# Softmax attention: the value products of two tiles issued as one block in every second step

## The chip, the cores and the metric

The kernel runs on one core of one Trainium2 chip. The metric is the device time of one execution, in microseconds (us). Five engines work side by side, each through its own instructions in the order in which the program issues them: PE (TensorE: matmuls and transposes, results in PSUM), DVE (VectorE), ACT (ScalarE), POOL (GpSimd) and SP (SyncE, which issues the DMAs here). They wait for each other through semaphores.

## The reference, cut to what matters

The whole computation is a chain of six residual blocks on `x` of shape (2, 1024, 128): a mixture of experts, a softmax attention, the same mixture again, a local attention with a feed-forward part, a linear attention, and the local block again. The change touches the softmax attention alone, with 16 heads of 64:

```python
qkv = (x @ qkv_w.T).reshape(Bb, Ss, 3, H, D)
q = _rope(q, c, s)
k = _rope(k, c, s)
scores = jnp.einsum('bhqd,bhkd->bhqk', q, k) * SCALE
dist = jnp.abs(pos[None, :] - pos[:, None])
kb = -p * jnp.log1p(a * dist)
attn = jax.nn.softmax(scores + kb[None], axis=-1)
out = jnp.einsum('bhqk,bhkd->bhqd', attn, v)
return out @ out_w.T
```

## The kernel before, in words

All data are float32. The attention (`attention0`, line 327) walks through 128 steps (line 737): four groups of four heads, two batches, two pairs of heads in a group, and eight tiles of 128 queries. One step is one pair of heads (r = 0 and 1) and one tile of queries against all 1024 keys. The 16 steps of one group and batch are called a block here. The loop (line 752) is a software pipeline written out by hand: nothing reorders it, so each engine gets its instructions in the order of the calls. In step i these calls are made, and each puts work on the engines named:

- `scores_of` (L642, PE): scores of step i. Each head's 1024 scores fill two banks of PSUM (`bank2`), and the two heads take all four banks of pool `psA`, so the scores of step i+1 can start in a bank only after step i's have been read from it.
- `weigh` (L709, PE): products of probabilities and values, for two query tiles at once (256 columns). The keys come in two halves, g = 0 and g = 1, of four key blocks; both halves add up in one bank, "O0". Half g = 0 of a pair of tiles is issued three steps behind the second tile's scores, and half g = 1 four steps behind. So an even step issues a g = 0, and the odd step after it the g = 1 of the same pair.
- `maxima` (L658, DVE): for each head, add the distance bias and take the row maximum, from PSUM into the tile `p`. It ends the use of the score banks.
- `raised` (L671, ACT): the exponential, in place in `p`, with the row sum in `den`.
- `turned` (L692 on PE, then L696 on ACT for head 0 or L698 on DVE for head 1): four 128x128 transposes of step i-2's `p` into one bank (`bankT`), and the copy of the bank into the tile `pt`, which `weigh` reads. A step makes four such calls, (g, r) = (0,0), (0,1), (1,0), (1,1). Pool `psT` has two banks, taken in turn: (1,0) takes the bank of (0,0) after ACT has copied it, and (1,1) takes the bank of (0,1) after DVE has copied it.
- `summed` (L723, ACT): copies the finished products of a pair of tiles from bank O0 into `at`.
- filler between the transposes (0,1) and (1,0): in steps divisible by 4 the output product `project` (L730 on PE, L734 on DVE); in the others one of twelve units for the next block, which are either rotary units (L590 on PE, L601 on DVE, L606 and L607 on POOL, DMAs of L611 on SP) or value projections (L620 on PE, L627 on ACT). In the last block (steps 112 to 127) no next block exists, and pieces of the next mixture of experts (`beside_last`) stand there instead, in some steps only.
- `scale_of` (L676 on DVE, L678 on POOL): divides `p` by its sum.

In 28 of the steps a part of the distance bias is made for a later pair of heads: a logarithm on ACT (L573) and a product on DVE (L574), both issued at the very head of the step. Of these steps 21 are odd (3, 5, 7, 27, 29, 31, 35, 37, 39 and so on) and 7 even.

Of the kernel before, what the change touches and what calls it, by code (L numbers as in the profile page):

```python
# [8 lines left out]
F32 = mybir.dt.float32  # L9
# [5 lines left out]
P = 128  # L15
# [16 lines left out]
def macaron_kernel(ctx: ExitStack, tc: tile.TileContext, a: dict, out: bass.AP):  # L32
    nc = tc.nc

    def pool(name, bufs, stack=ctx, **kw):
        return stack.enter_context(tc.tile_pool(name=name, bufs=bufs, **kw))
# [13 lines left out]
    def bankT(name):  # L50
        return psT.tile([P, 512], F32, tag="T", name=name)
# [3 lines left out]
    def bankO(name, which=None):  # L55
        if which is None:
            turn[0] ^= 1
            which = turn[0]
        return psO.tile([P, 512], F32, tag=f"O{which}", name=name)
# [253 lines left out]
    def beside_last(i):  # L313


        if i is None:
            first_weights()
            return
        for c, s in ((0, 0), (1, 5)):
            if 0 <= i - s < 10:  # L320
                lo, hi = ((0, 1), (1, 3), (3, 4), (4, 5), (5, 7), (7, 9), (9, 10), (10, 11), (11, 12), (12, 13))[i - s]
                for fn, *more in m1[1][3][lo:hi]:
                    fn(c, *more)
        for fn in m1[2][-(-len(m1[2]) * i // 16) : -(-len(m1[2]) * (i + 1) // 16)]:
            fn()

    def attention0():
        with ExitStack() as st:
# [306 lines left out]
            probs, nms, dens, pts, ats, avs = {}, {}, {}, {}, {}, {}  # L635
# [15 lines left out]
            def maxima(i, pss, hp, b, t, bias):  # L651

                o = 896 - t * P
                dens[i] = small.tile([P, 2], F32, tag="den", name=f"den_{hp}_{b}_{t}")
                nms[i] = small.tile([P, 2], F32, tag="nm", name=f"nm_{hp}_{b}_{t}")
                for r in range(2):
                    s = probs[i, r] = sp.tile([P, S], F32, tag="s", name=f"p_{hp}_{b}_{t}_{r}")
                    nc.vector.tensor_tensor_reduce(  # L658
                        out=s,
                        in0=pss[r].rearrange("p a n -> p (a n)"),  # L660
                        in1=bias[r][:, o : o + S],
                        scale=-1.0,
                        scalar=3.0e38,
                        op0=ALU.add,
                        op1=ALU.min,
                        accum_out=nms[i][:, r : r + 1],
                    )

            def raised(i, r):
                s, nm, den = probs[i, r], nms[i], dens[i]  # L670
                nc.scalar.activation(s, s, AF.Exp, bias=nm[:, r : r + 1], scale=-1.0, accum_out=den[:, r : r + 1])  # L671
# [8 lines left out]
            def turned(i, g, r, hp, b, t):  # L680

                q = t % 2
                if q == 0:
                    pts[i // 2, r, g] = work.tile(
                        [P, 4, 2 * P], F32, tag=f"pt{r}{g}", name=f"pt{r}{g}_{hp}_{b}_{t}", bufs=1 + g
                    )
                pt = pts[i // 2, r, g]
                s = probs[i, r]
                tp = bankT(f"tp_{hp}_{b}_{t}_{r}_{g}")
                for k in range(4):  # L690
                    kb = 4 * g + k
                    nc.tensor.transpose(tp[:, k * P : (k + 1) * P], s[:, kb * P : (kb + 1) * P], ident)  # L692
                dst = pt[:, :, q * P : (q + 1) * P]
                src = tp.rearrange("p (k n) -> p k n", n=P)
                if r == 0:
                    nc.scalar.copy(dst, src)  # L696
                else:
                    nc.vector.tensor_copy(dst, src)  # L698
                if g == 1:
                    probs.pop((i, r))  # L700

            def weigh(i, g, hp, b, t, v):

                if g == 0:
                    avs[i // 2] = bankO(f"av_{hp}_{b}_{t}", 0)
                po = avs[i // 2]
                for kb in range(4 * g, 4 * g + 4):
                    for r in range(2):
                        nc.tensor.matmul(  # L709
                            po[r * 64 : r * 64 + 64, 0 : 2 * P],  # L710
                            lhsT=v[:, kb, r * 64 : r * 64 + 64],
                            rhs=pts[i // 2, r, g][:, kb - 4 * g, :],
                            start=(kb == 0),
                            stop=(kb == TB - 1),
                        )
                for r in range(2):
                    pts.pop((i // 2, r, g))

            def summed(i, hp, b, t):
                if t % 4 == 1:  # L720
                    ats[i // 4] = work.tile([P, 4 * P], F32, tag="at", name=f"at_{hp}_{b}_{t}", bufs=1)
                o = 256 * (t % 4 == 3)
                nc.scalar.copy(ats[i // 4][:, o : o + 2 * P], avs.pop(i // 2)[:, 0 : 2 * P])  # L723

# [13 lines left out]
            blocks = {0: block_of(*order[0])}  # L738
            biases, making = {}, {}

            def bias_part(hp, r, *half):
                if hp not in biases:
                    biases[hp], making[hp] = bias_of(hp)
                making[hp](r, *half)
# [3 lines left out]
            work = pool("wk0", 2, st, reuse_waits="tile")  # L748
            sp = pool("sp0", 6, st, reuse_waits="tile")

            with tc.manual_schedule():
                for i in range(len(steps) + 8):
                    def of(d):
                        if 0 <= i - d < len(steps):
                            hg, b, j, t = steps[i - d]
                            return 2 * hg + j, b, t

                    if i == len(steps) - 16:
                        making_stack.close()
                        beside_last(None)  # L760
                    c, e = of(0), of(2)

                    if c:
                        hg, b, j, t = steps[i]
                        for hp, js, places in ((2 * hg + 2, (1, 1), (3, 5, 6, 7)), (2 * hg + 1, (0, 0), (3, 4, 5, 7))):
                            if (b, j) == js and t in places and (hg + 1 < H0 // 4 or not b):
                                k = places.index(t)
                                bias_part(hp, k // 2, slice(k % 2 * WIDE // 2, (k % 2 + 1) * WIDE // 2))
                        pss = scores_of(i, 0, *c, *blocks[i // 16][0][j]) if i else firsts

                    for d, g in ((3, 0), (4, 1)):
                        w = of(d)
                        if w and w[2] % 2 == 1:
                            weigh(i - d, g, *w, blocks[(i - d) // 16][1][w[0] % 2])
                    if c:
                        maxima(i, pss, *c, biases[c[0]])
                        raised(i, 0)
                    if e:
                        turned(i - 2, 0, 0, *e)
                    if c:  # L780
                        raised(i, 1)
                    w = of(4)
                    if w and w[2] % 2 == 1:
                        summed(i - 4, *w)
                    if e:
                        turned(i - 2, 0, 1, *e)

                    if i % 4 == 0 and of(8):
                        project(i - 8, *of(5))
                    elif i == 1:  # L790
                        ap2(0)
                        up2(0)
                        ap2(1)
                    elif 0 < i < len(steps):
                        n = i // 16 + 1
                        if i == 2:
                            up2(1)
                        if n < len(order) and n not in blocks:
                            blocks[n] = block_of(*order[n])
                        if n < len(order) and blocks[n][2]:  # L800
                            blocks[n][2].pop(0)()
                    if len(steps) > i >= len(steps) - 16:
                        beside_last(i - len(steps) + 16)
                    if e:
                        turned(i - 2, 1, 0, *e)
                        turned(i - 2, 1, 1, *e)
                    if c:
                        scale_of(i)
                    if i == 0:
                        rest_of_norm()  # L810
# [133 lines left out]
    work = pool("wk1", 1, reuse_waits="tile")  # L944
# [622 lines left out]
    _, left, finish, front_parts, pair_parts = m1[1]  # L1567
# [115 lines left out]
```

## Time and profile before

| what | value |
|---|---|
| time, median of 3 runs (lowest, highest) | 1916.71 us (1916.43, 1918.86) |
| the profiled execution: its time | 1920.34 us |
| the profiled execution: span from first to last instruction | 1918.6 us |
| mean granted TensorE clock | 0.986 |
| first and last score matmul of the attention (L642) | 135.2 and 990.4 us |
| DVE, ACT, POOL busy, share of the span | 73%, 59%, 59% |

In a timeline each row has the start in us from the span's start, the duration in us, the engine, the line, the operation, the tiles written and read with their shapes, and the number of instructions merged into the row. Brackets hold the idle time of the engine before the row and what ended it. A float32 matmul is issued as two instructions, a transpose as one: a step's four score matmuls are a row of x8, and one half of the value products (eight matmuls) is a row of x16. The ends of PE's rows are modelled and overlap the next start a little, so PE's time is best read from start to start.

### The profile page before, as it was taken

Reading aid. Unit: us, or ns where it says so; the run is one execution under the profiler, and the core shown is the slowest. Engines: PE = TensorE matmul, PEld = TensorE weight load, DVE = VectorE, ACT = ScalarE, POOL = GpSimd, SP = SyncE. Lnnn points to the kernel's source line nnn. Section 1 sums busy time; section 2 is a strip of 40 time slices with the busy share of each in tenths; the row PEclk is TensorE's granted clock in tenths of the full one; section 3 lists DMA queues with packets and bytes.
Section 4 is the critical chain, followed back from the end, with each engine's and each line's share of the span. In section 5 each row is a group of like instructions: output and inputs, shape, how many; then the busy total and the mean of one; then the engine's idle time right before and its main releaser. Section 6 shows DMA issues by size and latency. Waiting matters only on the chain.

```text
span 1918.6 us, 37580 instructions
## 1 busy us (share of the span) xinstructions
PE 1837.8 (96%) x14482; PEld 1190.8 (62%) x14482; DVE 1402.5 (73%) x2450; ACT 1131.1 (59%) x2083; POOL 1135.9 (59%) x1036
## 2 busy tenths in 40 slices
PE   8998999999999999999999888999999899999997
PEld 5554666566665666566566556666756566666665
DVE  5758677776778677776763568888887888888884
ACT  3335555655566555655653356776767467677765
POOL 4544444353434444344444379888887689788883
PEclk8998999999999999999999899999999999999999
DMA  5330101010101101012012111101100000011110
GB/s 132 106 88 23 23 12 34 12 24 11 34 12 23 23 16 30 12 32 62 2 61 98 63 39 29 26 20 29 26 18 15 6 18 18 21 26 24 26 34 26
DMA packets 52413, 64.13 MB, mean 33 GB/s; under 512 B 17890, under 2 KB 26892, under 8 KB 51980
## 3 DMA queue, kind: packets, MB, share of 16 engines
q1 hardware_dynamic: 52236, 61.74, 12.6%
q8 instruction: 115, 1.88, 0.4%
q14 instruction: 62, 0.51, 0.1%
HBM read 27.89 MB, written 1.31 MB: 15 GB/s over the span
## 4 chain that ended last, share of the span: by engine, by line
PE 66%; ACT 12%; DVE 12%; POOL 4%; issue 4%; DMA 0%; SPq 0%; DVEq 0%; POOLq 0%; ACTq 0%
PE s L642 10%; PE tp L692 10%; PE av L709 9%; ACT p L671 4%; PE qk_f L979 3%; PE gu_m L275 3%; PE gu_m L276 2%; PE av_f L1151 2%; PE s_f L1090 2%; PE pq L590 2%; PE tq_f L1046 2%; PE tp_f L1137 2%; PE acc_m L259 2%; PE v_f L1057 2%; PE po_f L1267 2%
## 5 line engine op out<-in xcount | busy, mean ns | idle before, releaser
L678 POOL TENSOR_SCALAR p<-p,den 128x1024 f32<-128x1024 f32 x256 | 293.3, 1160 | 402.8 <-DVE den L676 324.8
L671 ACT ACTIVATE p<-p,nm 128x1024 f32<-128x1024 f32 x256 | 294.7, 1151 | 357.5 <-DVE nm L658 343.9
L658 DVE CUSTOM_DVE_ANT_0 p<-s,bias 128x1024 f32<-128x1024 f32 x256 | 302.8, 1219 | 107.6 <-PE s L642 105.0
L692 PEld LDWEIGHTS tp<-ident,p 128*128 128x128 f32 x2048 | 225.6, 141 | 102.3 <-ACT pt L696 38.7
L692 PE MATMUL tp<-ident,p 128*128 128x128 f32 x2048 | 275.3, 277 | 13.6 <-ACT pt L696 12.8
L642 PE MATMUL s<-qk,qk 64*128 64x512 f32 x1024 | 258.5, 621 | 4.2 <-DVE nm L658 4.2
L709 PE MATMUL av<-pt,v 128*64 128x256 f32 x2048 | 249.0, 385 | 0.0
L698 DVE COPY pt<-tp 128x512 f32<-128x512 f32 x256 | 176.2, 688 | 90.9 <-PE tp L692 90.5
L709 PEld LDWEIGHTS av<-pt,v 128*64 128x64 f32 x2048 | 135.7, 136 | 150.1 <-issue 83.7
L1025 POOL TENSOR_TENSOR t_f<-t_f,t_f 128x1024 f32<-128x1024 f32 x64 | 151.2, 2363 | 15.3 <-DVE t_f L1011 12.5
L299 POOL TENSOR_TENSOR h_m<-h_m,cb_m 128x512 f32<-128x512 f32 x64 | 87.2, 1364 | 120.3 <-DVE h_m L295 90.5
L696 ACT COPY pt<-tp 128x512 f32<-128x512 f32 x256 | 147.7, 577 | 4.9 <-PE tp L692 4.7
L642 PEld LDWEIGHTS s<-qk,qk 64*128 64x128 f32 x1024 | 89.9, 188 | 87.3 <-issue 87.0
L1030 POOL TENSOR_TENSOR t_f<-t_f,rn_f 128x1024 f32<-128x1024 f32 x64 | 122.5, 1914 | 23.3 <-ACT rn_f L1021 23.2
L1129 POOL TENSOR_TENSOR s_f<-s_f,sm_f 128x1024 f32<-128x1024 f32 x64 | 121.7, 1901 | 15.5 <-DVE sm_f L1125 11.9
L979 PE MATMUL qk_f<-wqkv,hT 128*128 128x512 f32 x256 | 124.7, 610 | 2.5 <-DVE hh_f L1243 1.2
L992 ACT ACTIVATE t_f<-qk_f 128x1024 f32<-128x1024 f32 x64 | 65.4, 1022 | 97.7 <-PE qk_f L979 90.3
L291 ACT ACTIVATE h_m<-gu_m 128x512 f32<-128x512 f32 x72 | 43.0, 597 | 134.9 <-PE gu_m L276 127.8
L1115 POOL TENSOR_TENSOR s_f<-s_f,mx_f 128x1024 f32<-128x1024 f32 x64 | 122.2, 1910 | 0.5 <-DVE mx_f L1110 0.5
L295 DVE TENSOR_TENSOR h_m<-h_m,gu_m 128x512 f32<-128x512 f32 x72 | 49.2, 685 | 86.4 <-ACT h_m L291 86.3
L1124 DVE TENSOR_REDUCE sm_f<-s_f 128x8 f32<-128x1024 f32 x64 | 77.9, 1217 | 27.1 <-ACT s_f L1120 27.0
L1142 ACT COPY pt_f<-tp_f 128x512 f32<-128x512 f32 x128 | 68.5, 587 | 40.6 <-PE tp_f L1137 40.5
(375 smaller groups left out, 3738.4 us busy)
## 6 DMA issues: line engine op xcount, KB each, us to landing
cb_m<-cwd_m SPq DMA_DIRECT2D x128, 128.0 KB, 3.0
qk<-rot SPq DMA_DIRECT2D x256, 64.0 KB, 2.0
tab<-in_xpos_dram SPq DMA_DIRECT2D x2, 1024.0 KB, 6.5
wqkv<-in_L_ffn_wqkv_dram SPq DMA_DIRECT2D x2, 768.0 KB, 8.0
x<-in_L_attn_x_dram SPq DMA_DIRECT2D x4, 256.0 KB, 3.6
wraw<-in_qkv_wT_dram SPq DMA_DIRECT2D x2, 512.0 KB, 4.7
vb_f<-vo_f SPq DMA_DIRECT2D x8, 128.0 KB, 2.2
out_dram<-x SPq DMA_DIRECT2D x4, 256.0 KB, 2.3
```

The lines of the kernel that those rows point to most:

```text
L642: nc.tensor.matmul(pss[r][:, c, :], lhsT=qT[rows[r], t * P : (t + 1) * P], rhs=kT[rows[r], c * 512 : (c + 1) * 512], start=True, stop=True,)
L658: nc.vector.tensor_tensor_reduce(out=s, in0=pss[r].rearrange("p a n -> p (a n)"), in1=bias[r][:, o : o + S], scale=-1.0, scalar=3.0e38, op ...
L671: nc.scalar.activation(s, s, AF.Exp, bias=nm[:, r : r + 1], scale=-1.0, accum_out=den[:, r : r + 1])
L678: nc.gpsimd.tensor_scalar(probs[i, r], probs[i, r], den[:, r : r + 1], 1.0, ALU.mult, ALU.mult)
L692: nc.tensor.transpose(tp[:, k * P : (k + 1) * P], s[:, kb * P : (kb + 1) * P], ident)
L696: nc.scalar.copy(dst, src)
L698: nc.vector.tensor_copy(dst, src)
L709: nc.tensor.matmul(po[r * 64 : r * 64 + 64, 0 : 2 * P], lhsT=v[:, kb, r * 64 : r * 64 + 64], rhs=pts[i // 2, r, g][:, kb - 4 * g, :], star ...
L979: nc.tensor.matmul(ps[:, s, :], lhsT=hTs[b][:, n * P : (n + 1) * P], rhs=lw[l][0][:, s * INNER : (s + 1) * INNER], start=True, stop=True,)
L1025: nc.gpsimd.tensor_tensor(t1, t1, t2, ALU.add)
L1030: nc.gpsimd.tensor_tensor(t3, t3, rn.unsqueeze(2).to_broadcast([P, 2 * HL, 64]), ALU.mult)
L1115: nc.gpsimd.tensor_tensor(s3, s3, mx.unsqueeze(2).to_broadcast([P, HL, P]), ALU.subtract)
```

## The change

Both halves of the value products of a pair of tiles are issued in the same even step, three steps behind the second tile's scores, and the odd steps issue none. The copy `summed` moves with them, from the odd step to the even one. In an odd step, ACT's copy of the first transposes, (0,0), is issued ahead of the step's first exponential; in even steps it stays between the two exponentials. `pt` of half g = 1 has one buffer where it had two, and `at` two where it had one.

```diff
                     pts[i // 2, r, g] = work.tile(
-                        [P, 4, 2 * P], F32, tag=f"pt{r}{g}", name=f"pt{r}{g}_{hp}_{b}_{t}", bufs=1 + g
+                        [P, 4, 2 * P], F32, tag=f"pt{r}{g}", name=f"pt{r}{g}_{hp}_{b}_{t}", bufs=1
                     )
...
-                    ats[i // 4] = work.tile([P, 4 * P], F32, tag="at", name=f"at_{hp}_{b}_{t}", bufs=1)
+                    ats[i // 4] = work.tile([P, 4 * P], F32, tag="at", name=f"at_{hp}_{b}_{t}", bufs=2)
...
-                    for d, g in ((3, 0), (4, 1)):
-                        w = of(d)
-                        if w and w[2] % 2 == 1:
-                            weigh(i - d, g, *w, blocks[(i - d) // 16][1][w[0] % 2])
+                    w = of(3)
+                    if w and w[2] % 2 == 1:
+                        for g in range(2):
+                            weigh(i - 3, g, *w, blocks[(i - 3) // 16][1][w[0] % 2])
                     if c:
                         maxima(i, pss, *c, biases[c[0]])
+
+                    first = e and not (w and w[2] % 2 == 1)
+                    if first:
+                        turned(i - 2, 0, 0, *e)
+                    if c:
                         raised(i, 0)
-                    if e:
+                    if e and not first:
                         turned(i - 2, 0, 0, *e)
                     if c:
                         raised(i, 1)
-                    w = of(4)
                     if w and w[2] % 2 == 1:
-                        summed(i - 4, *w)
+                        summed(i - 3, *w)
                     if e:
                         turned(i - 2, 0, 1, *e)
```

## The prediction

> **What bounds the kernel now.** I read the page first, then the timeline of one plain step, then that of steps which lack a part, because there the next limit shows. The page says that PE is busy nearly throughout, and that the chain which ended last runs through it for two thirds; the attention's three PE lines lead that chain.
>
> ```profile
> PE 1837.8 (96%) x14482; PEld 1190.8 (62%) x14482; DVE 1402.5 (73%) x2450; ACT 1131.1 (59%) x2083; POOL 1135.9 (59%) x1036
> ```
>
> A busy PE is no proof that PE sets the pace, so here are PE's rows and DVE's main ones in one odd step (85), in order of time:
>
> ```profile
> 708.37 1.99 PE L642 MATMUL s<-qk,qk 64*128 64x512 f32 x8
> ...
> 710.28 1.95 PE L709 MATMUL av<-pt,v 128*64 128x256 f32 x16
> 710.49 1.23 DVE L658 CUSTOM_DVE_ANT_0 p<-s,bias 128x1024 f32<-128x1024 f32 x1 [1.26 <-PE s L642]
> ...
> 711.64 1.22 DVE L658 CUSTOM_DVE_ANT_0 p<-s,bias 128x1024 f32<-128x1024 f32 x1
> ...
> 712.16 1.09 PE L692 MATMUL tp<-ident,p 128*128 128x128 f32 x8
> ...
> 713.09 1.02 PE L590 MATMUL pq<-xnT_a,wqk 128*128 128x512 f32 x2
> 713.29 0.69 DVE L698 COPY pt<-tp 128x512 f32<-128x512 f32 x1 [0.42 <-PE tp L692]
> ...
> 713.95 1.04 PE L692 MATMUL tp<-ident,p 128*128 128x128 f32 x8
> ...
> 714.92 1.99 PE L642 MATMUL s<-qk,qk 64*128 64x512 f32 x8
> ```
>
> From start to start PE spends 1.91 us on scores, 1.88 on half of the value products, 0.93 on transposes (0,0) and (0,1), 0.86 on the filler and 0.97 on (1,0) and (1,1): 6.55 us with no gap. DVE and ACT follow: both heads' maxima run from T+2.12 to T+4.5 (T is the start of the step's scores), beside the value products and the first transposes, and DVE even waits 1.26 us for the scores. So the value products are the cover under which DVE takes its maxima. The change takes this cover out of the odd steps.
>
> The trace has a step without cover already: step 3, before the first products.
>
> ```profile
> 160.50 1.99 PE L642 MATMUL s<-qk,qk 64*128 64x512 f32 x8
> ...
> 162.42 1.09 PE L692 MATMUL tp<-ident,p 128*128 128x128 f32 x8
> ...
> 163.34 1.20 DVE L658 CUSTOM_DVE_ANT_0 p<-s,bias 128x1024 f32<-128x1024 f32 x1
> ...
> 164.48 1.21 DVE L658 CUSTOM_DVE_ANT_0 p<-s,bias 128x1024 f32<-128x1024 f32 x1
> ...
> 165.62 0.68 DVE L698 COPY pt<-tp 128x512 f32<-128x512 f32 x1
> ...
> 165.80 0.56 ACT L696 COPY pt<-tp 128x512 f32<-128x512 f32 x1
> ...
> 166.41 1.09 PE L692 MATMUL tp<-ident,p 128*128 128x128 f32 x8 [2.04 <-ACT pt L696]
> ...
> 167.44 1.99 PE L642 MATMUL s<-qk,qk 64*128 64x512 f32 x8
> ```
>
> Here PE stands for 2.04 us ahead of (1,0) and (1,1): the two `psT` banks are full until ACT has copied (0,0), at 166.36, and DVE (0,1), at 166.30. DVE comes to its copy only behind both maxima, in program order. The step takes 6.94 us though it has 1.88 us less work than its neighbours.
>
> **The change, part by part.**
>
> *The second half joins the first in even steps.* It brings 16 more instructions of L709 in a row. The tail of the attention has such a row of 32 in the trace of before:
>
> ```profile
> 1004.90 3.67 PE L709 MATMUL av<-pt,v 128*64 128x256 f32 x32
> ...
> 1008.50 0.71 PE L730 MATMUL pj<-wo,at 128*128 128x128 f32 x4
> ```
>
> That is 3.60 us for 32 against 1.88 for 16, so the second half costs 1.72: one turn from products to transposes, 0.16 us, is saved in each pair of steps. An even step of 6.57 becomes about **8.28**. Its inputs are there: head 0's copy of (1,0) by ACT and head 1's of (1,1) by DVE are the last work of the odd step and end about T+0.9 and T+1.4 of the even one, by adding up their rows; the second half starts at T+3.8. The maxima, from T+2.13 to T+4.5, lie beside the longer products.
>
> *The odd step loses 1.88 us of PE work.* If PE were the only limit, it would take 1.92 + 0.92 + 0.86 + 0.97 = 4.67 us (scores to transposes takes 1.92 too, by step 3). But (1,1) needs the bank of (0,1). Maxima start at T+2.13 (scores must have ended), the second 1.15 later, DVE's copy 1.14 after that, at T+4.42; it takes 0.69, PE starts (1,1) 0.06 later, at T+5.17, and the next scores come 0.58 after such a late start (in step 116, (1,1) alone starts at 921.74 and scores at 922.32). The odd step takes **5.75 us**, and PE waits about 1.1 us of it. That is the wait which the change adds; queued behind it on PE are the next scores, and behind them everything. The score banks themselves are free at T+4.5, so they would not hold PE.
>
> *ACT's copy of (0,0) moved ahead of the exponential* in odd steps ends by about T+3.2, before head 0's maximum lets the exponential start at T+3.45; it costs nothing. It takes ACT out of the wait that step 3 shows. What is late next is DVE's copy, 0.06 us earlier there and left where it was.
>
> *`summed`*, 0.35 us of ACT, moves from odd to even steps, where ACT has the room. *Buffers*: the single `pt` of g = 1 is written again at about T+8 of the even step and last read at T+5.5; the second `at` lets `summed` write while `project` still has to read the old one. Neither costs. The orders of POOL and SP are untouched, and no DMA moves. POOL's scaled `p` of an odd step is ready over 5 us before its transposes (step 85: 719.62 against 725.3); odd steps will start them 1.9 us earlier, which is still in time.
>
> *Bias steps.* In 20 odd steps from 5 on, the logarithm (L573) and product (L574) stand ahead of the maxima, which now start at T+2.59 (step 29), 2.87 (step 5) or 3.69 (step 31). Today most of that delay lies under the products; then it adds to the odd step one for one: 0.46 to 1.56 us over T+2.13. I take 0.85, near the two lower rows: **6.6 us** a step.
>
> *Last block.* Steps without filler take 6.26 now and show the same wait in small: transposes start at 906.12, DVE copies (0,1) from 907.25 to 907.94, the next scores start at 908.58. Its odd steps have the same floor of 5.75.
>
> **The sum**, steps 4 to 127, now 167.44 to 995.60, 828.2 us (124 steps, mean 6.68):
> 54 even steps x 8.28 = 447.1; 34 plain odd x 5.75 = 195.5; 20 odd with bias x 6.6 = 132.0; the last block's 8 even, now 53.5, plus 8 x 1.72 = 67.2; its 8 odd x 5.75 plus 2.5 for the mixture's pieces (step 121 now takes 1.7 more than its neighbours) = 48.5. Together 890.3, which is **62 us more**. Step 3 gains 0.5, since its ACT copy comes early. The profiled execution took 1920.3, so 1982; it lies 3.6 above the median of the three runs, hence **1978 us** against 1916.7.
>
> The bounds: bias delay of 0.46 or 1.56 in all 20 steps, -8 or +14; no saved turn (1.88 in place of 1.72), +10; mixture's pieces free, -2.5. That gives 1967 to 2002.
>
> A rule weighed: after step 3's idle time of 2.04 us the scores took their usual 1.99, and the granted clock of that step was 1.00; after 4.2 us idle (140 to 144 us) the clock of the stretch fell, 0.82 on the mean, and scores at 151.89 took 3.23. The Trainium skill, "TensorE: Matmul & The Clock Gate", section "Why this matters for your kernels", asks for no idle gap over about 3 us, and its "Part 4: PE-mode transpose" says that transposes don't count as busy in the same way. By the first the new gaps of 1 to 2 us are harmless; by the second a last-block odd step, with nothing but transposes and waiting from T+1.9 to T+5.75, could be throttled, and the sum would grow as in the second rival below.
>
> **The rivals.**
> 1. *PE alone sets the pace, and the change is faster.* This holds if (1,1) does not wait for DVE: pair 8.28 + 4.67 = 12.95 against 13.14, 62 pairs, -12 us, and up to -12 more from bias waits of today that vanish (steps 30 and 31 take 7.8 each): about 1900. It decides at an odd step of 4.86, that is with DVE's copy done by T+4.2; the rows give T+5.1. For it speaks only that DVE's waits don't show ahead of L692 in plain steps; against it step 3 and the 6.26 us steps.
> 2. *The wait also lowers the clock.* Idle of 2.04 us left it at 1.00, 4.2 us did not; the last block's odd steps idle some 1.9. With scores at 3.23, +1.24 in 8 steps gives 1988, in all 62 odd steps 2055.
> 3. *The wait is partly hidden*, because DVE gets through the odd step faster than its rows add up: with half the wait, about 1945. I see no row for it.
>
> **How the numbers follow.** Forecast 0.80; rival 1 0.05; rival 2 and other added waits 0.10; rival 3 0.05. The range 1957 to 2005 takes the bounds above and some of rivals 2 and 3. Faster by over 0.2% (about what a measurement of this kernel can tell from no change): 0.05; within: 0.01; slower: 0.94.
>
> **What would show it.** Starts of L642 alternate between steps of about 8.3 and 5.75 us; in odd steps PE idles about a microsecond ahead of the last transposes, released by DVE L698; L709 comes in rows of 32 that take 3.6; the clock stays at 1.00. The forecast is wrong if odd steps take 4.7 (rival 1), or if scores after them take over 2 us (rival 2).

## The result, and the profile after

| | before | changed |
|---|---|---|
| time, median of 4 runs (lowest, highest) | 1917.78 us (1916.43, 1919.55) | 1974.64 us (1972.27, 1976.60) |
| ratio to before, with its 95% interval | | 1.0293 (1.028 to 1.0305) |
| span of the profiled execution | 1918.6 us | 1973.5 us |
| mean granted TensorE clock | 0.986 | 0.986 |

The change makes the kernel 2.9% slower. On the page of the changed kernel PE's busy time is what it was; its share fell because the span grew. The row of the transposes (busy time, mean of one, then idle time just ahead and what ended most of it) shows what PE waits for. Before, this row had 13.6 us of idle time, most of it ended by ACT's copy:

```profile
L692 PE MATMUL tp<-ident,p 128*128 128x128 f32 x2048 | 275.3, 277 | 13.6 <-ACT pt L696 12.8
```

Now it has 69.0 us, nearly all of it ended by DVE's copy:

```profile
PE 1837.5 (93%) x14482; PEld 1194.6 (61%) x14482; DVE 1391.7 (71%) x2450; ACT 1141.3 (58%) x2083; POOL 1135.9 (58%) x1036
...
L692 PE MATMUL tp<-ident,p 128*128 128x128 f32 x2048 | 288.3, 278 | 69.0 <-DVE pt L698 66.6
```

The changed kernel's timeline, one odd step (79) and the head of the even one after it (start, duration, engine, line, tiles, count, idle time ahead):

```profile
701.60 1.99 PE L642 MATMUL s<-qk,qk 64*128 64x512 f32 x8
...
703.51 1.09 PE L692 MATMUL tp<-ident,p 128*128 128x128 f32 x8
703.73 1.23 DVE L658 CUSTOM_DVE_ANT_0 p<-s,bias 128x1024 f32<-128x1024 f32 x1 [1.26 <-PE s L642]
...
704.88 1.22 DVE L658 CUSTOM_DVE_ANT_0 p<-s,bias 128x1024 f32<-128x1024 f32 x1
...
706.02 0.69 DVE L698 COPY pt<-tp 128x512 f32<-128x512 f32 x1
...
706.76 0.66 PE L692 MATMUL tp<-ident,p 128*128 128x128 f32 x4 [0.82 <-DVE pt L698]
...
707.35 1.99 PE L642 MATMUL s<-qk,qk 64*128 64x512 f32 x8
...
709.27 3.67 PE L709 MATMUL av<-pt,v 128*64 128x256 f32 x32
...
712.87 1.09 PE L692 MATMUL tp<-ident,p 128*128 128x128 f32 x8
```

The odd step takes 5.75 us, from 701.60 to 707.35. Transposes (1,1), the row of x4, stand alone behind a wait: DVE copies (0,1) from 706.02 to 706.71, only when both maxima are done, and PE goes on at 706.76. The even step has its 32 product instructions in a row, 3.60 us from start to start. Before, a plain step took 6.55 to 6.59 us, and the same copy stood in nobody's way.

By the starts of L642 the loop divides as follows; the first column of numbers is the prediction's sum:

| steps | predicted, us | measured, us |
|---|---|---|
| 54 even (4 to 110) | 447.1 | 448.2 (8.30 each) |
| 34 odd without bias part | 195.5 | 195.5 (5.75 each) |
| 20 odd with bias part | 132.0 | 127.9 (6.40 each) |
| 8 even of the last block | 67.2 | 69.1 |
| 8 odd of the last block | 48.5 | 48.3 |
| sum; more than before (828.2) | 890.3; +62.1 | 889.0; +60.8 |

Around these steps the changed kernel gained. Step 4 starts at 164.34 and not 167.44, 3.1 us earlier: 1.9 us of that lie in steps 2 and 3, and 1.2 ahead of step 0. From the start of L730's last row to the end it took 905.2 us, not 908.7. That figure lay between 903.7 and 908.7 in the nine kernels of this study, and the start of step 0 between 133.9 and 136.3 in those that leave step 0 as it was. These kernels are the same there, so neither is an effect of the change that these runs can show. 60.8 + 0.6 (the steps behind 127) - 3.1 - 3.5 gives 54.8 of the 54.9 us between the spans.

### The profile page after: what moved, and what is told of

Its sections match the earlier page's. It is cut to its first block, busy times and chain, and to the rows that moved or that the text cites. A ratio compares the mean times of both kernels' runs of the same rounds, so it can differ in the third digit from the quotient of the medians.

```text
span 1973.5 us, 37674 instructions
## 1 busy us (share of the span) xinstructions
PE 1837.5 (93%) x14482; PEld 1194.6 (61%) x14482; DVE 1391.7 (71%) x2450; ACT 1141.3 (58%) x2083; POOL 1135.9 (58%) x1036
## 3 DMA queue, kind: packets, MB, share of 16 engines
HBM read 27.89 MB, written 1.31 MB: 15 GB/s over the span
## 4 chain that ended last, share of the span: by engine, by line
PE 63%; DVE 16%; ACT 9%; issue 6%; POOL 5%; DMA 1%; DVEq 0%; POOLq 0%; ACTq 0%
PE av L709 11%; PE s L642 10%; PE tp L692 7%; DVE p L658 5%; PE qk_f L983 3%; PE gu_m L275 3%; PE gu_m L276 2%; PE av_f L1155 2%; PE s_f L1094 2%; DVE pt L698 2%; PE tq_f L1050 2%; PE acc_m L259 2%; PE tp_f L1141 2%; PE po_f L1271 2%; PE v_f L1061 2%
## 5 line engine op out<-in xcount | busy, mean ns | idle before, releaser
L692 PE MATMUL tp<-ident,p 128*128 128x128 f32 x2048 | 288.3, 278 | 69.0 <-DVE pt L698 66.6
L642 PE MATMUL s<-qk,qk 64*128 64x512 f32 x1024 | 260.4, 625 | 4.2 <-DVE nm L658 4.2
L709 PE MATMUL av<-pt,v 128*64 128x256 f32 x2048 | 235.5, 383 | 0.0
L709 PEld LDWEIGHTS av<-pt,v 128*64 128x64 f32 x2048 | 141.6, 137 | 112.8 <-issue 48.3
L642 PEld LDWEIGHTS s<-qk,qk 64*128 64x128 f32 x1024 | 90.2, 188 | 87.7 <-issue 87.3
L291 ACT ACTIVATE h_m<-gu_m 128x512 f32<-128x512 f32 x72 | 43.0, 597 | 132.0 <-PE gu_m L276 123.0
L606 POOL TENSOR_TENSOR rot<-rot,rot 128x512 f32<-128x512 f32 x32 | 40.7, 1272 | 100.7 <-DVE rot L601 100.6
```

The costliest lines, as they stand in the source:

```text
L642: nc.tensor.matmul(pss[r][:, c, :], lhsT=qT[rows[r], t * P : (t + 1) * P], rhs=kT[rows[r], c * 512 : (c + 1) * 512], start=True, stop=True,)
L709: nc.tensor.matmul(po[r * 64 : r * 64 + 64, 0 : 2 * P], lhsT=v[:, kb, r * 64 : r * 64 + 64], rhs=pts[i // 2, r, g][:, kb - 4 * g, :], star ...
```

## The experiments

The theory on trial: the odd step is a chain of scores, both maxima, DVE's copy of (0,1), transposes (1,1). The rivals: the score banks, ACT, the bias parts' own cost, or the clock. All edits are to the changed kernel, unless another is named. Ratios are to the kernel before, run beside them.

### A bank of its own for (0,1) in odd steps (e1_spare_bank)

```diff
-                tp = bankT(f"tp_{hp}_{b}_{t}_{r}_{g}")
+                tp = bankO(f"tp_{hp}_{b}_{t}_{r}_{g}", 0) if (q, r, g) == (1, 1, 0) else bankT(f"tp_{hp}_{b}_{t}_{r}_{g}")
```

> The changed kernel, but in odd steps the transposes (0,1) go to bank O0, which holds no products in odd steps; so (1,1) needn't wait until DVE has copied (0,1). Theory (the odd step of 5.75 us is scores, two maxima, DVE's copy of (0,1), then (1,1)): plain odd steps fall to PE's own sum, 1.92 + 0.92 + 0.86 + 0.97 = 4.67 us, just above the 4.5 us at which the score banks come free; the 20 odd steps with a bias part, now 6.40 on the mean, to about 5.2 (their score banks come free later); the last block's odd steps to about 4.6. 34 x -1.08, 20 x -1.2 and 8 x -1.15 make -70 us: about 1905 us, less than the kernel before. Rival (the copy isn't what holds PE: the score banks, ACT or a lower clock do): no change, 1975 us.

Measured: 1908.87 us, ratio 0.9954 (0.9939 to 0.9969). The timeline of this kernel in odd step 85:

```profile
702.74 1.09 PE L692 MATMUL tp<-ident,p 128*128 128x128 f32 x8
...
703.67 1.02 PE L590 MATMUL pq<-xnT_a,wqk 128*128 128x512 f32 x2
...
704.53 1.04 PE L692 MATMUL tp<-ident,p 128*128 128x128 f32 x8
705.24 0.69 DVE L698 COPY pt<-tp 128x512 f32<-128x512 f32 x1
...
705.49 1.99 PE L642 MATMUL s<-qk,qk 64*128 64x512 f32 x8
```

(1,0) and (1,1) are one row of x8 again, and (1,1) runs ahead of the copy of (0,1), which starts at 705.24. Plain odd steps take 4.67 to 4.71 us, as PE's own sum says. One bank undoes the whole loss and turns it into a small gain over the kernel before. In the steps around a bias part the wait showed up elsewhere than expected: the odd steps stay at 4.67 to 4.95, where about 5.2 was expected, and the even steps behind them take 8.6 to 9.45, since their scores start and then wait for the second head's bank (in step 28 the scores take 2.6 us and not 1.99, and the second maximum ends 0.6 us behind their start).

### The copy of (0,1) between the two maxima (e2_copy_between)

```diff
...
                     if c:
-                        maxima(i, pss, *c, biases[c[0]])
+                        maxima(i, pss, *c, biases[c[0]], rs=(0,) if first else (0, 1))
                     if first:
                         turned(i - 2, 0, 0, *e)
+                        turned(i - 2, 0, 1, *e)
+                    if c and first:
+                        maxima(i, pss, *c, biases[c[0]], rs=(1,))
...
-                    if e:
+                    if e and not first:
                         turned(i - 2, 0, 1, *e)
```

> The changed kernel, but in odd steps DVE copies (0,1) between the two maxima and not behind both. Theory: (1,1) is free to start by T+4.15, but the second maximum, and with it the second head's score banks, ends 0.69 us later, at T+5.2; so the next limit shows, the score banks. Odd steps of 5.1 to 5.3 us, 62 x -0.55 = -34 us: about 1940 us, between the changed kernel and the one before. Rival 1 (only the copy of (0,1) counts, the score banks never do): odd steps of 4.67, about 1907. Rival 2 (DVE's copy is not the releaser): 1975 or more, since the maxima only come later.

Measured: 1944.84 us, ratio 1.0135 (1.012 to 1.0151). This kernel's timeline in odd step 79, which starts at 683.54 (the edit moves lines: L693 and L699 are the transposes and DVE's copy, L659 the maxima):

```profile
686.82 0.69 DVE L699 COPY pt<-tp 128x512 f32<-128x512 f32 x1
...
687.28 1.04 PE L693 MATMUL tp<-ident,p 128*128 128x128 f32 x8
687.42 1.21 DVE L659 CUSTOM_DVE_ANT_0 p<-s,bias 128x1024 f32<-128x1024 f32 x1
...
688.25 2.43 PE L642 MATMUL s<-qk,qk 64*128 64x512 f32 x8
```

The wait at (1,1) is gone, and the next limit shows where the theory put it: the second maximum now ends at 688.6, while the scores of the next step start at 688.25 and stretch to 2.43 us where they took 1.99, so they hold a wait for the second head's banks. By starts of L642 the odd step is 4.7 and the even one 8.76 us, 13.46 the pair against 14.05. So with the copy moved up the score banks are the next limit, and cost some 0.5 us a pair over the 12.97 of e1_spare_bank.

### ACT's copy of (0,0) left late (e3_act_copy_late)

```diff
-                    first = e and not (w and w[2] % 2 == 1)
+                    first = False
```

> The changed kernel, but ACT's copy of (0,0) stands behind the first exponential in odd steps too, as in even ones. Theory: two copies hold PE in an odd step, and each alone costs nearly the whole wait. ACT's copy then ends at about T+5.15, (1,0) and (1,1) follow it together, and the next scores 1.03 later: odd steps of 6.2 us, 62 x +0.47 = +29 us, about 2004 us. Rival (moving ACT's copy bought nothing, as DVE's copy ends at the same time): no change, 1975 us.

Measured: 2026.27 us, ratio 1.0575 (1.0554 to 1.0596). Plain odd steps take 6.24 us, as expected, so moving ACT's copy is worth about 0.5 us a step and is no part of the loss. The total lies 22 us over the expectation. The timeline of odd step 71, which has a bias part and starts at 668.50, up to the scores of step 72:

```profile
673.87 0.56 ACT L696 COPY pt<-tp 128x512 f32<-128x512 f32 x1
...
674.49 1.72 PE L692 MATMUL tp<-ident,p 128*128 128x128 f32 x7 [2.11 <-ACT pt L696]
...
676.36 2.77 PE L642 MATMUL s<-qk,qk 64*128 64x512 f32 x8
```

PE waits 2.11 us, and then transposes and scores run slow: the granted clock is 0.50 from 674 to 678 us. There were ten such falls between step 5 and the end of the loop. This is the prediction's second rival, in a kernel that waits longer. The last two experiments look into it.

### All bias parts in even steps (e4_bias_even)

```diff
-                        for hp, js, places in ((2 * hg + 2, (1, 1), (3, 5, 6, 7)), (2 * hg + 1, (0, 0), (3, 4, 5, 7))):
+                        for hp, js, places in ((2 * hg + 2, (1, 1), (0, 2, 4, 6)), (2 * hg + 1, (0, 0), (0, 2, 4, 6))):
```

> The changed kernel, but all bias parts stand at the head of even steps (tiles 0, 2, 4, 6), under the longer products. Theory: their delay of the maxima is hidden there, so the 20 odd steps which take 6.40 on the mean fall to 5.75 and even steps stay at 8.3: -13 us, about 1962 us. Rival (the bias parts cost the time of ACT or DVE as such, or share a memory port with POOL, wherever they stand): no change, 1975 us.

Measured: 1965.88 us, ratio 1.0245 (1.023 to 1.026), 9 us less than the changed kernel. All odd steps from 5 to 111 take 5.75 but one of 6.10, and the even ones stay at 8.28 to 8.32: 12.6 us less in steps 4 to 111, as the theory has it. Some of this is lost outside: step 0 now makes a bias part and takes 10.15 instead of 9.07, the loop began later, and the clock fell twice in the last block.

### Both together (e5_both)

The edits of e1_spare_bank and e4_bias_even.

> The spare bank for (0,1) in odd steps, and all bias parts at the head of even steps. Theory: with the spare bank, the even steps behind a bias part take 0.3 to 1.2 us longer than the others (the late maxima then hold the score banks), 13.6 us in all by that run's steps; with the bias parts under the long products this goes, so 1908.9 - 13.6, and about 1 us back for the part that lands in step 0: about 1896 us, 1.1% below the kernel before. Rival (DVE's work of an odd step now runs 2.2 us into the even one, so a bias part in an even step is no longer hidden): no change, 1909 us or more.

Measured: 1896.48 us, ratio 0.9885 (0.987 to 0.9899): 1.2% faster than the kernel before. Odd steps of 4.67 to 4.71 and even ones of 8.28 to 8.32 alternate with one exception (step 60, 8.59) from step 4 to step 111. So the long even steps of e1_spare_bank came from the bias parts in the odd steps, and DVE's overhang into the even step hides too. What moving the bias parts would do to the kernel before was not measured, so how much of the 1.2% is the bunching's is not shown.

### Work in the wait: a matmul (e6_late_matmul), or transposes (e7_late_transposes)

Both edits are to the kernel with ACT's late copy, ahead of (1,0). The result is read by nothing.

```diff
+                    if c and i % 2 and i > 4:
+                        spare = bankO(f"spare_{i}", 0)
+                        nc.tensor.matmul(
+                            spare, lhsT=ident, rhs=wo[:, 0:4, :].rearrange("p j m -> p (j m)"), start=True, stop=True
+                        )
```

> The kernel with ACT's late copy, and one matmul of 128x512 into the idle bank O0 in every odd step from 5 on, ahead of (1,0), whose result nothing reads. That kernel took 2026 us where the sum of its waits gave 2004, and its granted clock fell to 0.50 ten times between steps 5 and 127, for some 3.5 us each, always behind an odd step with a long wait of PE; each costs about 1.3 us. The added matmul takes 0.86 us and fits into the wait of 1.35 to 2.1 us, so it costs nothing itself. Theory (the clock follows how long PE does matmuls in a window): the falls go, about 2013 us. Rival (the falls have another cause): 2026 us with ten falls, or more if the matmul isn't hidden (62 x 0.86 = +53).

In the other kernel the matmul is replaced:

```diff
+                        for k in range(8):
+                            nc.tensor.transpose(spare[:, k % 4 * P : (k % 4 + 1) * P], ident, ident)
```

> As the kernel with the added matmul, but with eight transposes in its place, which take PE the same 0.86 us in each odd step and are read by nothing. If transposes keep the clock up as matmuls do: as that kernel, no falls, about 2013 us. If the clock doesn't count them: about ten falls to 0.50 as without them, about 2026 us.

Measured: 2010.62 us with the matmul, ratio 1.0481 (1.0463 to 1.0498), and 2008.88 us with the transposes, 1.0473 (1.0457 to 1.0489). More work, and 16 to 17 us less time than without it. From step 5 to the end of the loop the clock fell once in the first kernel and never in the second, against ten times. Steps 4 to 126 took 927.8 us without the added work, 915.0 with the matmul and 912.3 with the transposes. The mean granted clock of all four runs agrees: 0.975 to 0.978 without, 0.984 to 0.988 with. Plain odd steps take 6.24 us as before, so the added work lies wholly in the wait. The timeline of the second kernel in an odd step of the last block (113), where L811 is the added work:

```profile
977.73 1.09 PE L692 MATMUL tp<-ident,p 128*128 128x128 f32 x8
978.66 1.04 PE L811 MATMUL spare<-ident 128*128 128x128 f32 x8
981.03 1.09 PE L692 MATMUL tp<-ident,p 128*128 128x128 f32 x8 [1.34 <-ACT pt L696]
982.05 1.99 PE L642 MATMUL s<-qk,qk 64*128 64x512 f32 x8
```

For 4.3 us PE has nothing but transposes and a wait of 1.34, and the scores behind them still take their full-clock 1.99 us.

## Why the prediction was right, point by point

- **The added wait was right, in place and size.** PE waits for DVE's copy of (0,1), 0.82 us by PE's row in step 79 and 1.08 by the length of the step (5.75 against the 4.67 of PE's own sum), and plain odd steps take 5.75 us as worked out. That it is this copy, and not the banks of the scores, ACT or the clock, is shown by e1_spare_bank: another bank for (0,1) alone takes 66 us off. e2_copy_between, which moves the copy up in DVE's order, takes off 30 us and shows what comes next.
- **The even step was right**: 8.30 against 8.28. 32 products in a row take 3.60 us, one turn saved.
- **The cost of nothing for ACT's early copy was right**, and the copy is needed: without it odd steps take 6.24 (e3_act_copy_late).
- **The bias parts were mis-sized.** The step of the sum was 0.85 us of delay in 20 odd steps; they measured 6.40 - 5.75 = 0.65, or 4 us less in all. The loop's sum is closer than its parts, by luck: the even steps took 1.1 us more than forecast and the last block's even steps 1.9 more, 1.6 of it in the one that a fall of the clock made longer (rival 2). The step which I had taken as the far bound, 31, had maxima at T+3.69 before and has them at T+2.67 now (358.04 to 360.71); the product L574 took 1.62 us there before, 0.72 now. That the parts cost by standing in the short steps, and not in themselves, is shown by e4_bias_even.
- **Steps 2 and 3** gave back 1.9 us and not 0.5; step 3 alone 1.3 (6.94 to 5.64), for (1,0) no longer waits, so that only half of the transposes stand behind the copy.
- **Rival 1** fell: odd steps at 4.67 with even ones at 8.30 exist only with a free bank (e1_spare_bank, e5_both). Its price of about 1900 was near for that case: 1909, and 1896 with the bias parts moved.
- **Rival 2** was real but small here. The changed kernel's clock fell once in the loop, behind odd step 113 in the last block, and even step 114 took 9.63 us, where step 118, which also lacks a filler, took 7.99:

```profile
949.43 0.66 PE L692 MATMUL tp<-ident,p 128*128 128x128 f32 x4 [1.26 <-DVE pt L698]
...
950.02 3.28 PE L642 MATMUL s<-qk,qk 64*128 64x512 f32 x8
```

- **Rival 3** fell: no part of the wait is hidden in plain steps.

## What to carry to other kernels

Work that is "only" on the busiest engine may be the cover of another engine's chain. Before bunching it, work out the step that is left without it: here scores, two maxima and one copy in DVE's order are longer than PE's rest, and with two banks in turn the longer chain sets the step. When the bunching itself saves something (here one turn per pair of steps), look for the resource that it leaves idle: the products' bank is empty in the very steps that lack a bank, and with it the same change is faster than the kernel before.

## What the runs showed of the hardware that was not expected

The clock falls at shorter waits than the trace of before had shown: there 2.04 us of idle time left it at 1.00 and 4.2 us did not. In e3_act_copy_late nine of the ten falls to 0.50 stand behind one wait of 2.1 to 2.5 us, the tenth behind one of 1.41; in the changed kernel one of 1.26 did it, behind transposes. Each of these falls lasted 3.41 us. A stretch of the changed kernel's windows (busy time and count of PE, PEld, DVE, ACT and POOL, then clock, DMA share and GB/s):

```profile
951.00:953.40 2.40, 2.40 (x8) 0.52 (x6) 0.00 (x0) 0.00 (x0) 2.31 (x3) 0.50 0.00 0
```

Other waits of the same length had no fall: in steps 5 to 126 of e3_act_copy_late, eight of 17 waits over 2.05 us. Part of the difference is where a wait lies. In each trace all falls of the run begin whole multiples of 3.413 us apart, as on a fixed raster (643.84 and 674.56 in e3_act_copy_late are nine apart). Nine of that kernel's ten falls follow a stretch of the raster in which PE was busy for 1.31 us or less, and no stretch of its loop without a fall had less than 1.46:

```profile
578.99:582.40 3.41, 1.46 (x14) 1.27 (x11) 3.41 (x6) 1.59 (x3) 2.67 (x3) 1.00 0.42 96
671.15:674.56 3.41, 1.30 (x7) 0.47 (x6) 3.41 (x7) 1.84 (x4) 1.32 (x1) 1.00 0.00 0
```

At 674.56, where the second row ends, the clock falls; at 582.40 it stays at 1.00. So a wait counts by how much of one such stretch it fills. That is not the whole rule: the tenth fall follows 2.00 us of busy time and the changed kernel's fall 1.91, while 1.75 (619.47 to 622.88 in the changed kernel) had no fall. What else decides stays open.

In these runs work put into the wait kept the clock up, and transposes did so as well as a matmul: ten falls became one with a matmul of 0.86 us and none with eight transposes of the same time, and useless work made that kernel 16 to 17 us faster. The Trainium skill, "TensorE: Matmul & The Clock Gate", "Part 4: PE-mode transpose", says that transposes don't count as busy in the same way; for these float32 transposes the runs show no sign of such a difference. Its rule of no idle gap over about 3 us ("Why this matters for your kernels") would have passed the waits of 2.1 us behind which the clock fell.
